# The expert-choice feed-forward of a four-layer decoder: layernorm rows and router products of three token groups moved beside the cross-attention, and the threshold search done on a transposed table

## The chip, the cores and the metric

The kernel is one launch on one core of a Trainium2 chip. The time is the device time of that core in microseconds (us), and lower is better. The core has five engines that run side by side and wait for each other by semaphores: TensorE (PE, with its weight loads as PEld), VectorE (DVE), ScalarE (ACT), GpSimd (POOL) and SyncE (SP, which here only issues transfers). Transfers between the core's memory and the chip's main memory run on 16 DMA engines.

## The reference

The whole program is a decoder of four layers on 16 sequences of 128 tokens (2048 tokens) of width 256. Each layer adds three parts to the running value `x`, each on the layernorm of `x`: a mixer, a cross-attention to a context, and a feed-forward. The change touches the third layer (number 2) only: the end of its cross-attention and its feed-forward, a mixture of 8 experts in which each expert chooses its 256 tokens:

```python
def _L2_ffn_ref(x, Wg, W1, W2):
    B, S, D = x.shape
    E = Wg.shape[1]                 # 8
    T = B * S                       # 2048
    cap = max(1, T // E)            # 256
    xt = x.reshape(T, D)
    logits = xt @ Wg
    probs = jax.nn.softmax(logits, axis=-1)
    pT = probs.T
    _, top_idx = jax.lax.top_k(pT, cap)
    sel = jnp.zeros((E, T), dtype=bool).at[jnp.arange(E)[:, None], top_idx].set(True)
    masked = jnp.where(sel, pT, -jnp.inf)
    assigned = sel.any(axis=0)
    tok2exp = jnp.where(assigned, jnp.argmax(masked, axis=0), jnp.argmax(pT, axis=0))
    weights = jnp.take_along_axis(probs, tok2exp[:, None], axis=1)[:, 0]
    out = jnp.zeros_like(xt)
    for e in range(E):
        gate = jnp.where(tok2exp == e, weights, 0.0)
        h = jax.nn.gelu(xt @ W1[e], approximate=False) @ W2[e]
        out = out + gate[:, None] * h
    return out.reshape(B, S, D)
...
x = x + _L2_xattn_ref(_layernorm(x, axis=-1), ctx_768, ...)     # 8 heads of 64
x = x + _L2_ffn_ref(_layernorm(x, axis=-1), L2_ffn_Wg, L2_ffn_W1, L2_ffn_W2)
```

An expert's choice is the same as a threshold: its 256 largest probabilities are those at or above the 256th largest, with ties settled by the order of the tokens.

## The kernel before

`x` stays on the core in four tiles `x[g]`, one for each group of four sequences (512 tokens: 4 blocks `t` of 128 tokens by 256). The parts of the layers are methods called in order, and a scheduler orders each engine's instructions by their dependences; matrix products issued through `pinned` and `pinned_transpose` (L253 to L258) keep their program order.

The cross-attention `l2_xattn` is `xattn64` (L919) with 8 heads: 16 units `m`, one for each block of tokens. For a unit it issues on PE, all pinned, the column sums `d` of the exponentials of the unit before, the scores `st`, the values `o`, the spread of the reciprocals `rb`, then the maxima's scores `s` of the next unit and the output product `proj` of the unit before the last. `add_x` (L220) adds `proj` to `x`. Every fourth unit a `prologue` makes keys, queries and values of the next group. `xattn64` takes a function `begin`, which is called after the weights are loaded and gives back a table of functions to be called at the ends of units. Layer 1's cross-attention passes `l1_ffn_begin`, which puts layernorm statistics (`stats`), rows (`rows`) and transposes (`turn`) of its feed-forward beside the units in this way. Layer 2's passes nothing.

The feed-forward `l2_ffn` (L1658) runs these stages one after the other:

1. Set-up: 23 transfers of 128 KB write zeros to `hs` in main memory (L1675, queue of SP), and POOL fills constants, among them `bits`, the candidates' bit patterns (L1684).
2. Logits: for each group a layernorm (`norm_tokens`, L194 to L205, rows into `hall`), eight transposes of 128x128 (`tr`, L183), two copies out of PSUM (`hT`, L110 and L112), and for each block two products with Wg (`logits`, L166), which give 8 columns for 128 tokens.
3. Softmax over 8 experts (L1714 to L1721), as `p3`, 128 tokens x (16 blocks x 8 experts).
4. Search: the threshold's bits are found two at a time in 15 rounds. A round makes three candidates for each expert (`cand`, L1732), compares all of `p3` with them (`mask`, L1735: 3 x 16 x 8 = 384 columns), sums over the 128 partitions with a product by ones (`count` on PE), sums over the 16 blocks (`count`, L1743), compares with the capacity (L1744), adds the bits up (`step`, L1746) and sets them (`thr`, L1747). Each step waits for the one before.
5. Selection: `ranks` (L1750) gives each chosen token a running number, with four shifted additions on DVE and two kinds of product on PE; it is called for the tokens above the threshold, for those equal to it, and for the tokens' experts `oh`. What comes out is a row number `at` for each token and an expert for each block of 128 rows.
6. Scatter: 16 indirect transfers on POOL write the rows of `hall` to `hs` (L1827).
7. Blocks: 23 blocks of 128 rows. `fetch` (L1837) reads four blocks of `hs` in one transfer of 512 KB when `b % 4 == 0` (`hb`, L1841, queue of ACT), and an expert's weights for each block (1 MB, queue of SP), into seven buffers of 8 KB per partition (`slot`, L116), which are also those of the cross-attention's weights. Then two transposes (`htr`), the first product, Gelu, four transposes and the second product.
8. Gather: 16 indirect transfers bring the rows back and DVE adds them to `x` (L1902, L1906).

Of the kernel before, what the change touches and what calls it, by code (L numbers as in the profile page):

```python
# [8 lines left out]
F = mybir.dt.float32  # L9
BF = mybir.dt.bfloat16  # L10
U32 = mybir.dt.uint32
AF = mybir.ActivationFunctionType
ALU = mybir.AluOpType
AX = mybir.AxisListType
PSUM = bass.MemoryType.PSUM

P = 128
B = 16
T = B * P
DM = 256  # L20
DC = 192
NG = 4
GB = B // NG
GT = GB * P
# [5 lines left out]
class Decoder:  # L30
# [1622 lines left out]
                add(last, t, po[t] if t < 2 else project(last, t))  # L1653

    def l2_xattn(self):
        self.xattn64(8, [f"L2_xattn_{n}" for n in ("Wq", "Wk", "Wv", "Wout")], "L2_xattn_bout", "l2x")

    def l2_ffn(self):  # L1658

# [2 lines left out]
        nc = self.nc  # L1662
        E, CAP = 8, T // 8
        NB = B + E - 1
        I32 = mybir.dt.int32
        wg = self.wp.tile([P, 2, E], F, tag="wg2", name="wg2")
        self.load_into(wg, "L2_ffn_Wg")
        hs = self.tc.dram_tile([NB * P, DM], F, name="hs")
        ys = self.tc.dram_tile([NB * P, DM], F, name="ys")
        with self.tc.tile_pool(name="l2f", bufs=1) as wk:  # L1670
            tile_ = lambda shape, name, dt=F, bufs=1: wk.tile(shape, dt, tag=name, name=name, bufs=bufs)
            zero = tile_([P, DM], "zero")
            nc.gpsimd.memset(zero, 0.0)
            for b in range(NB):
                nc.sync.dma_start(out=hs[b * P : (b + 1) * P, :], in_=zero)  # L1675
            onesb = tile_([P, P], "onesb", BF)
            nc.gpsimd.memset(onesb, 1.0)
            upb = tile_([P, P], "upb", BF)
            nc.gpsimd.tensor_copy(upb, self.tri["up"])

            bits = tile_([P, 15, 3, E], "bits", I32)
            for i in range(15):
                for j in range(3):
                    nc.gpsimd.memset(bits[:, i, j, :], (j + 1) << (2 * i))  # L1684
            eight = tile_([P, E], "eight")
            for n in range(E):
                nc.gpsimd.memset(eight[:, n : n + 1], float(E - n))
# [9 lines left out]
            for r in ends:  # L1697
                nc.gpsimd.memset(r[:, 0:4], 0.0)

            h = tile_([P, B, DM], "hall")  # L1700
            logits = self.b1("logits")[:, 0 : B * E]
            for g in range(NG):
                hg = h[:, g * GB : (g + 1) * GB, :]
                self.norm_tokens(self.x[g], hg)
                hT = self.hidden_T(hg)
                for t in range(GB):
                    o = (g * GB + t) * E
                    self.mm(logits[:, o : o + E], [(hT[:, k, t * P : (t + 1) * P], wg[:, k, :]) for k in range(2)])

            p3 = tile_([P, B, E], "p3")  # L1710
            flat = lambda a: a.rearrange("p t e -> p (t e)")
            m = self.small([P, B], "m16")
            l3 = logits.rearrange("p (t e) -> p t e", e=E)
            nc.vector.tensor_reduce(m, l3, AX.X, ALU.max)  # L1714
            bcast = lambda a: a.unsqueeze(2).to_broadcast([P, B, E])
            over_t = lambda a: a.unsqueeze(1).to_broadcast([P, B, E])
            nc.vector.tensor_tensor(p3, l3, bcast(m), ALU.subtract)
            nc.scalar.activation(flat(p3), flat(p3), AF.Exp)
            nc.vector.tensor_reduce(m, p3, AX.X, ALU.add)
            nc.vector.reciprocal(m, m)  # L1720
# [1 line left out]

            thr = tile_([P, E], "thr", I32)
            nc.vector.memset(thr, 0)
            cand = tile_([P, 3, E], "cand", I32)
            mask = tile_([P, 3, B, E], "mask", BF)
            count = tile_([P, 3, E], "count")
            step = tile_([P, E], "step", I32)  # L1730
            for i in range(14, -1, -1):
                nc.vector.tensor_tensor(  # L1732
                    cand, bits[:, i], thr.unsqueeze(1).to_broadcast([P, 3, E]), ALU.bitwise_or
                )
                nc.vector.tensor_tensor(  # L1735
                    mask,
                    p3.unsqueeze(1).to_broadcast([P, 3, B, E]),
                    cand.bitcast(F).unsqueeze(2).to_broadcast([P, 3, B, E]),
                    ALU.is_ge,
                )  # L1740
                ps = self.b1("count")[:, 0 : 3 * B * E]
                self.mm(ps, [(onesb, mask.rearrange("p j t e -> p (j t e)"))])
                nc.vector.tensor_reduce(count, ps.rearrange("p (j t e) -> p j e t", j=3, e=E), AX.X, ALU.add)  # L1743
                nc.vector.tensor_scalar(count, count, CAP - 0.5, float(1 << (2 * i)), ALU.is_ge, ALU.mult)  # L1744
                with nc.allow_low_precision(reason="whole numbers of two bits"):
                    nc.vector.tensor_reduce(step, count.rearrange("p j e -> p e j"), AX.X, ALU.add)  # L1746
                nc.vector.tensor_tensor(thr, thr, step, ALU.bitwise_or)  # L1747
            thrf = over_t(thr.bitcast(F))

            def ranks(mask):  # L1750

# [11 lines left out]
            equal = tile_([P, B, E], "equal", BF)  # L1763
            nc.vector.tensor_tensor(above, p3, thrf, ALU.is_gt)
            nc.vector.tensor_tensor(equal, p3, thrf, ALU.is_equal)
            _, n = ranks(above)
            rest = self.small([P, E], "rest8")
            nc.vector.tensor_scalar(rest, n, -1.0, float(CAP), ALU.mult, ALU.add)
            rank, _ = ranks(equal)
# [55 lines left out]
            moves = []  # L1825
            for t in range(B):
                i = nc.gpsimd.indirect_dma_start(  # L1827
                    hs[:, :], bass.IndirectOffsetOnAxis(ap=at[:, t : t + 1], axis=0), h[:, t, :], None
                )
                for j in moves:  # L1830
                    self.tc.declare_no_dep(i.ins, j.ins, reason="the rows of different tokens are different")
                moves.append(i)
# [2 lines left out]
            hbs, hTs, ws, yTs = {}, {}, {}, {}  # L1835

            def fetch(b):  # L1837
                if b % 4 == 0:
                    k = min(4, NB - b)
                    hbs[b // 4] = wk.tile([P, 4, DM], F, tag="hb", name="hb", bufs=3)  # L1840
                    nc.scalar.dma_start(  # L1841
                        out=hbs[b // 4][:, 0:k, :], in_=hs[b * P : (b + k) * P, :].rearrange("(b p) d -> p b d", p=P)
                    )
                e = nc.sync.value_load(ebi[0:1, b : b + 1], min_val=0, max_val=E - 1)
                w = self.slot([P, 2, 1024], "W12")
                w1 = w[:, 0, :].rearrange("p (c f) -> p c f", c=2)
                w2 = w[:, 1, :].rearrange("p (c d) -> p c d", c=4)
                nc.sync.dma_start(
                    out=w1, in_=self.a["L2_ffn_W1"][bass.ds(e, 1)].rearrange("o (c p) f -> p (o c) f", p=P)
                )  # L1850
                nc.sync.dma_start(
                    out=w2, in_=self.a["L2_ffn_W2"][bass.ds(e, 1)].rearrange("o (c p) d -> p (o c) d", p=P)
                )
                ws[b] = w1, w2

            def tokens(b):
                ps = self.b1("htr")[:, 0:DM]
                for k in range(2):
                    self.pinned_transpose(ps[:, k * P : (k + 1) * P], hbs[b // 4][:, b % 4, k * P : (k + 1) * P])
                hTs[b] = wk.tile([P, 2, P], F, tag="hTs", name="hTs", bufs=3)  # L1860
                nc.vector.tensor_copy(hTs[b].rearrange("p c n -> p (c n)"), ps)

# [548 lines left out]
```

## Time and profile before

| What | us |
|---|---|
| Median of 3 runs (3657.71, 3664.07, 3664.17) | 3664.07 |
| The profiled execution's own time | 3659.25 |
| Its span | 3657.5 |
| PE busy | 3343.9 (91% of the span) |
| DVE busy | 2115.8 (58%) |
| ACT busy | 1426.7 (39%) |
| POOL busy | 457.2 (12%) |
| From the last `add_x` of layer 2's cross-attention (2266.37) to the first step of the softmax (2291.68) | 25.31 |
| The 15 rounds of the search (2295.02 to 2333.64) | 38.6 |
| From the end of the search to the row numbers (2346.72) | 13.1 |
| From the row numbers to the first transpose of a block (2374.92) | 28.2 |

The page gives, for one execution, each engine's busy time, the span in 40 slices, the chain of work that ended last, followed back from the end, and groups of equal instructions. Times within the span are us from its start. In the chain and the timeline a row is: start, duration, engine, tile and line, and how many instructions are merged. Durations of PE are modelled, so the start of the next instruction that waits for it is the safer figure. In a table by windows, the columns are the busy time (and number) of PE, PEld, DVE, ACT and POOL, then the TensorE clock that was granted (1.00 is full), the DMA share and GB/s.

### The profile page before, as it was taken

How to read it: one execution, taken by the hardware profiler on the slowest of the kernel's cores; microseconds unless marked ns; L12 is line 12 of the kernel's file. 1: busy time of each engine (PE TensorE's matmuls, PEld its weight loads, DVE VectorE, ACT ScalarE, POOL GpSimd, SP SyncE). 2: the span in 40 equal slices, each digit the busy share in tenths (PEclk: the TensorE clock that was granted, in tenths of full speed). 3: DMA queues.
4: the chain of work that ended last, by engine and by line, in shares of the span. 5: the costliest groups of instructions: out<-in, count | busy, mean ns of one | idle time of the engine just before them, and what ended most of it. 6: DMA issues, size and time to landing. Idle time of an engine off the chain costs nothing.

```text
span 3657.5 us, 51423 instructions
## 1 busy us (share of the span) xinstructions
PE 3343.9 (91%) x20959; PEld 1806.8 (49%) x20976; DVE 2115.8 (58%) x4133; ACT 1426.7 (39%) x1917; POOL 457.2 (12%) x627
## 2 busy tenths in 40 slices
PE   7888999999998899997799999196999999999999
PEld 4655555555556556664455567062122222224656
DVE  6545444444463534468677644425799999973440
ACT  2344411111124422238455422023477777783221
POOL 5423100000003311110010110104100000002100
PEclk9978999999999999999999999597799999999989
DMA  3000000000110100010000001273312020000000
GB/s 98 4 7 1 14 20 20 18 22 18 32 48 2 38 1 1 1 42 8 12 1 12 2 1 34 105 250 107 60 25 31 11 31 11 11 1 25 1 8 18
DMA packets 90484, 105.46 MB, mean 29 GB/s; under 512 B 11364, under 2 KB 72678, under 8 KB 89990
## 3 DMA queue, kind: packets, MB, share of 16 engines
q1 hardware_dynamic: 79672, 89.71, 9.3%
q0 software_dynamic: 4224, 6.43, 0.5%
q10 hardware_dynamic: 6352, 6.03, 0.5%
q8 instruction: 165, 2.70, 0.3%
q14 instruction: 71, 0.58, 0.1%
HBM read 85.53 MB, written 16.60 MB: 28 GB/s over the span
## 4 chain that ended last, share of the span: by engine, by line
PE 79%; DVE 10%; ACT 5%; issue 3%; POOL 2%; DMA 1%; SPq 0%; POOLq 0%; ACTq 0%; DVEq 0%
PE acc L1943 7%; PE down L255 6%; PE gate L255 6%; PE up L255 6%; PE proj L255 6%; PE st L1943 5%; PE one L1943 4%; PE qT L166 4%; PE st L255 4%; PE o L255 2%; PE h L255 2%; DVE mx L2089 2%; PE rb L255 2%; PE v L948 2%; PE pr L166 2%
## 5 line engine op out<-in xcount | busy, mean ns | idle before, releaser
L2089 DVE TENSOR_REDUCE mx<-one 128x1 f32<-128x512 f32 x1024 | 659.0, 686 | 61.8 <-PE one L1943 52.7
L2226 ACT ACTIVATE e<-st 128x1024 f32<-128x1024 f32 x512 | 497.0, 1021 | 214.1 <-PE st L1943 213.0
L674 ACT ACTIVATE gs<-gate,cols 128x512 f32<-128x512 f32 x132 | 90.7, 687 | 552.6 <-PE gate L255 552.6
L1943 PE MATMUL acc<-e,v 128*32 128x512 f32 x2048 | 288.9, 613 | 0.9 <-ACT e L2226 0.9
L1943 PE MATMUL st<-qp,kp 113*128 113x512 bf16 x1024 | 273.8, 388 | 3.4 <-ACT e L2226 1.9
L688 DVE SCALAR_TENSOR_TENSOR x<-down,w_all,x 128x256 f32<-128x256 f32 x512 | 212.4, 477 | 111.1 <-PE down L255 110.9
L255 PE MATMUL down<-expert,gs 128*128 128x256 f32 x1056 | 251.0, 381 | 2.2 <-DVE gs L675 2.2
L255 PE MATMUL gate<-hT,expert 128*128 128x512 f32 x528 | 250.3, 596 | 0.0
L255 PE MATMUL up<-hT,expert 128*128 128x512 f32 x528 | 248.7, 593 | 0.0
L255 PEld LDWEIGHTS down<-expert,gs 128*128 128x128 f32 x1056 | 201.5, 191 | 86.1 <-issue 61.5
L675 DVE SCALAR_TENSOR_TENSOR gs<-up,cols,gs 128x512 f32<-128x512 f32 x132 | 99.0, 750 | 229.8 <-PE up L255 229.8
L1943 PE MATMUL one<-kp,qp 16*128 16x512 bf16 x1024 | 211.7, 399 | 4.0 <-DVE mx L2089 2.6
L1943 PEld LDWEIGHTS <-qp 16*128 16x128 bf16 x1024 | 49.0, 91 | 332.4 <-issue 327.0
L255 PEld LDWEIGHTS up<-hT,expert 128*128 128x128 f32 x528 | 100.8, 191 | 127.1 <-issue 126.9
L1943 PEld LDWEIGHTS <-kp 113*128 113x128 bf16 x1024 | 79.1, 98 | 141.8 <-issue 81.8
L1048 ACT COPY rb<-rb 128x512 f32<-128x512 f32 x64 | 37.5, 586 | 258.9 <-PE rb L255 258.9
L255 PEld LDWEIGHTS gate<-hT,expert 128*128 128x128 f32 x528 | 100.4, 192 | 70.5 <-issue 64.0
L1050 DVE TENSOR_TENSOR cT<-o,rb 128x512 f32<-128x512 f32 x64 | 44.3, 692 | 157.0 <-ACT rb L1048 157.0
L166 PE MATMUL qT<-hT,L_xattn_Wq 128*128 128x512 f32 x256 | 115.8, 606 | 6.6 <-DVE hT L110 4.5
L1346 DVE SCALAR_TENSOR_TENSOR xs<-xBC,cols,xs 128x508 f32<-128x508 f32 x144 | 106.1, 742 | 22.4 <-ACT xs L1342 19.0
L255 PE MATMUL o<-e,v 128*32 128x128 f32 (+1 forms) x2048 | 105.7, 280 | 11.8 <-DVE nm L292 11.8
L962 POOL CAST kb<-kT 128x512 bf16<-128x512 f32 x64 | 41.5, 677 | 433.9 <-DVE kT L110 433.9
(519 smaller groups left out, 5507.9 us busy)
## 6 DMA issues: line engine op xcount, KB each, us to landing
W<-in_L_ffn_W_dram SPq DMA_DIRECT2D x46, 512.0 KB, 5.5
expert<-in_L_ffn_Wg_dram SPq DMA_DIRECT2D x32, 128.0 KB, 2.2
expert<-in_L_ffn_Wu_dram SPq DMA_DIRECT2D x32, 128.0 KB, 2.7
expert<-in_L_ffn_Wd_dram SPq DMA_DIRECT2D x32, 128.0 KB, 2.4
parts<-parts SPq DMA_DIRECT2D x16, 256.0 KB, 2.3
qp<-parts SPq DMA_DIRECT2D x28, 128.0 KB, 3.8
kp<-parts SPq DMA_DIRECT2D x12, 256.0 KB, 8.3
hs<-zero SPq DMA_DIRECT2D x23, 128.0 KB, 1.9
```

Source lines behind the costliest of these rows:

```text
L166: self.nc.tensor.matmul(out, lhsT, rhs, start=i == 0, stop=i == n - 1 and bias is None)
L255: self.tc.keep_in_program_order(self.nc.tensor.matmul(*a, **k))
L674: nc.scalar.activation(gs, pg, AF.Silu, bias=bg)
L675: nc.vector.scalar_tensor_tensor(gs, pu, bu, gs, ALU.add, ALU.mult)
L688: nc.vector.scalar_tensor_tensor(xt, pd[:, t, :], w_all[:, o : o + 1], xt, ALU.mult, ALU.add)
L948: nc.tensor.matmul(ps, l, r, start=True, stop=False)
L962: nc.gpsimd.tensor_copy(kb[:, i + j, :], kT[:, i + j, :])
L1050: nc.vector.tensor_tensor(cT, po, rb, ALU.mult)
L1346: stt = lambda *a: pin(nc.vector.scalar_tensor_tensor(*a))
L1943: self.tc.keep_in_program_order(nc.tensor.matmul(*a, **k))
L2089: nc.vector.tensor_reduce(mx[:, t, kc, i : i + 1], pair[i], AX.X, ALU.max)
L2226: nc.scalar.activation(e[:, 2 * p : 2 * p + 2, :], ps, AF.Exp, scale=1.0 / 16.0)
```

## The change

Three groups' rows and logits move into the cross-attention's units through a new `l2_ffn_begin`; the fourth group follows after it (`st["last"]`). Each group's logits are now made turned: one product with Wg as the stationary operand, padded to 32 columns, gives 32 rows x 512 tokens in `lT`, a strip for each group, and four transposes bring all groups' logits back. The zeroing of `hs` moves there too. `hall` becomes two of the seven 8 KB buffers. The search works on `pT`, the transpose of `p3` (partition = block and expert, columns = 128 tokens): the counts come out of the comparisons themselves (`accum_out`), and one small product with `same` adds up the partitions of one expert. The thresholds come back by a transpose. The first of the three `ranks` becomes one product and one sum. `fetch` reads block 0 alone first, then four at a time. An `Exp` of a constant, whose result is not used, is issued ahead of the softmax.

```diff
     def l2_xattn(self):
-        self.xattn64(8, [...], "L2_xattn_bout", "l2x")
+        self.xattn64(8, [...], "L2_xattn_bout", "l2x", self.l2_ffn_begin)
+
+    def l2_ffn_begin(self):
+        ...
+        wg = self.wp.tile([P, 2, 32], F, tag="wg2", name="wg2")
+        nc.gpsimd.memset(wg, 0.0)
+        nc.sync.dma_start(out=wg[:, :, 0:E], in_=self.a["L2_ffn_Wg"].rearrange("(c p) n -> p c n", p=P))
+        zero = self.hp.tile([P, DM], F, tag="hT", name="zero", bufs=5)
+        nc.gpsimd.memset(zero, 0.0)
+        ...
+        for b in range(NB):
+            nc.sync.dma_start(out=hs[b * P : (b + 1) * P, :], in_=zero)
+        h = [self.slot([P, 8, DM], "hall") for _ in range(2)]
+        ...
+        def stats(gs):
+            ...
+            for i, g in enumerate(gs):
+                for t in range(GB):
+                    nc.vector.bn_stats(bs[:, t, :], self.x[g][:, t, :])
+                    nc.vector.bn_aggr(mv[:, i, t, :], bs[:, t, :])
+            self.rsqrt(rs, mv[:, :, :, 1])
+            ...
+        def rows(g):
+            mv, rs = vals[g]
+            for t in range(GB):
+                nc.vector.tensor_scalar(
+                    h[g // 2][:, g % 2 * GB + t, :], self.x[g][:, t, :], mv[:, t, 0:1], rs[:, t : t + 1], ALU.subtract, ALU.mult
+                )
+
+        def logits(g):
+            hT = self.hp.tile([P, 2, GT], F, tag="hT", name="hT", bufs=5)
+            for k in range(2):
+                ps = self.b1("tr")
+                for t in range(GB):
+                    self.pinned_transpose(ps[:, t * P : (t + 1) * P], h[g // 2][:, g % 2 * GB + t, k * P : (k + 1) * P])
+                self.evac(hT[:, k, :], ps)
+            r = slice(32 * g, 32 * g + 32)
+            ps = self.b1("lT")
+            for k in range(2):
+                self.pinned(ps[r, :], wg[:, k, :], hT[:, k, :], start=k == 0, stop=k == 1)
+            ...
+            nc.scalar.copy(st["lT"][r, :], ps[r, :])
+
+        st["last"] = [lambda: stats([3]), lambda: rows(3), lambda: logits(3)]
+        at = lambda f, *a: lambda: f(*a)
+        return {
+            10: [at(stats, [0, 1]), at(rows, 0)],
+            11: [at(rows, 1), at(logits, 0)],
+            12: [at(logits, 1)],
+            14: [at(stats, [2]), at(rows, 2)],
+            15: [at(logits, 2)],
+        }
...
     def l2_ffn(self):
...
-            bits = tile_([P, 15, 3, E], "bits", I32)
+            bits = tile_([P, 15, 3], "bits", I32)
             for i in range(15):
                 for j in range(3):
-                    nc.gpsimd.memset(bits[:, i, j, :], (j + 1) << (2 * i))
+                    nc.gpsimd.memset(bits[:, i, j : j + 1], (j + 1) << (2 * i))
+
+            m8 = tile_([P, E], "m8")
+            nc.vector.tensor_reduce(m8, self.ident.rearrange("p (t e) -> p e t", e=E), AX.X, ALU.add)
+            same = tile_([P, B, E], "same")
+            nc.gpsimd.tensor_copy(same, m8.unsqueeze(1).to_broadcast([P, B, E]))
...
-            for g in range(NG):
-                hg = h[:, g * GB : (g + 1) * GB, :]
-                self.norm_tokens(self.x[g], hg)
-                hT = self.hidden_T(hg)
-                for t in range(GB):
-                    o = (g * GB + t) * E
-                    self.mm(logits[:, o : o + E], [(hT[:, k, t * P : (t + 1) * P], wg[:, k, :]) for k in range(2)])
+            for work in self.l2f["last"]:
+                work()
+            ...
+            early = self.small([P, 1], "dy")
+            nc.scalar.activation(early, self.eps, AF.Exp)
+            lT = self.l2f["lT"]
+            ps = self.b1("logits")
+            for t in range(GB):
+                self.pinned_transpose(ps[:, t * P : (t + 1) * P], lT[:, t * P : (t + 1) * P])
...
+            ps = self.b1("pT")[:, 0:P]
+            self.pinned_transpose(ps, flat(p3))
+            pT = tile_([P, P], "pT")
+            nc.vector.tensor_copy(pT, ps)
+
+            best = tile_([P, 4], "best")
+            nc.vector.memset(best, 0.0)
+            thr = best[:, 3:4]
...
             for i in range(14, -1, -1):
-                nc.vector.tensor_tensor(
-                    cand, bits[:, i], thr.unsqueeze(1).to_broadcast([P, 3, E]), ALU.bitwise_or
-                )
-                nc.vector.tensor_tensor(mask, p3..., cand..., ALU.is_ge)
-                ps = self.b1("count")[:, 0 : 3 * B * E]
-                self.mm(ps, [(onesb, mask.rearrange("p j t e -> p (j t e)"))])
-                nc.vector.tensor_reduce(count, ps.rearrange("p (j t e) -> p j e t", j=3, e=E), AX.X, ALU.add)
-                nc.vector.tensor_scalar(count, count, CAP - 0.5, float(1 << (2 * i)), ALU.is_ge, ALU.mult)
-                ...
-                    nc.vector.tensor_reduce(step, count.rearrange("p j e -> p e j"), AX.X, ALU.add)
-                nc.vector.tensor_tensor(thr, thr, step, ALU.bitwise_or)
-            thrf = over_t(thr.bitcast(F))
+                nc.vector.tensor_tensor(cand, bits[:, i], thr.bitcast(I32).to_broadcast([P, 3]), ALU.bitwise_or)
+                for j in range(3):
+                    nc.vector.tensor_scalar(
+                        mask, pT, cand.bitcast(F)[:, j : j + 1], 0.0, ALU.is_ge, ALU.add, accum_out=count[:, j : j + 1]
+                    )
+                ps = self.b1("count")[:, 0:3]
+                self.pinned(ps, flat(same), count, start=True, stop=True)
+                nc.vector.scalar_tensor_tensor(best[:, 0:3], ps, CAP - 0.5, cand.bitcast(F), ALU.is_ge, ALU.mult)
+                nc.vector.tensor_reduce(thr, best, AX.X, ALU.max)
+            ps = self.b1("thr")[:, 0:P]
+            self.pinned_transpose(ps, thr.to_broadcast([P, P]))
+            thrf = ps.rearrange("p (t e) -> p t e", e=E)
...
-            _, n = ranks(above)
+            ps = self.b1("above")[:, 0 : B * E]
+            self.mm(ps, [(onesb, flat(above))])
+            n = self.small([P, E], "rest8")
+            nc.vector.tensor_reduce(n, ps.rearrange("p (t e) -> p e t", e=E), AX.X, ALU.add)
...
             def fetch(b):
-                if b % 4 == 0:
-                    k = min(4, NB - b)
+                if b == 0 or b % 4 == 1:
+                    k = min(4, NB - b) if b else 1
```

## The prediction

> **What bounds the kernel now.** The page's first part puts PE at 91% of the span, but its clock row falls to 5 tenths in the slice from 2286 to 2377, which holds most of the change's stages. The chain of waits, asked from 2225 to 2420, shows three regimes. Up to 2266 it is almost all PE: the cross-attention's unit repeats every 6.48 us (starts of `d` at 2142.09, 2148.57, 2155.05), and only one late table load, at 2253.81, adds 0.43. So a PE instruction put there costs its own time. From 2266.37 (last `add_x`) to 2374.92 it runs through one instruction after another, and each removed step pays in full. From 2375 to 2475 it is PE again, at 4.10 us a block; the change alters nothing there but the first fetch.
>
> Chain of waits; the logits of the last group end here, 25.31 us after the last `add_x`:
> ```profile
> 2288.06 3.60 PE logits L166 x16
> 2291.66 0.02 issue
> 2291.68 0.30 DVE m L1714
> ```
> Timeline of one round of the search (start, duration, engine, line). No engine overlaps another, and the next `cand` starts 2.57 us later; 15 rounds are 38.6 us:
> ```profile
> 2299.96 0.18 DVE L1732 TENSOR_TENSOR cand<-bits,thr 128x24 int32<-128x24 int32 x1
> 2300.18 0.56 DVE L1735 TENSOR_TENSOR mask<-p,cand 128x384 bf16<-128x384 f32 x1
> 2300.79 0.48 PE L166 MATMUL count<-mask,onesb 128*128 128x384 bf16 x1 [2.09 <-DVE mask L1735]
> 2301.30 0.56 DVE L1743 TENSOR_REDUCE count<-count 128x24 f32<-128x384 f32 x1 [0.57 <-PE count L166]
> 2301.90 0.18 DVE L1744 TENSOR_SCALAR count<-count 128x24 f32<-128x24 f32 x1
> 2302.11 0.18 DVE L1746 TENSOR_REDUCE step<-count 128x8 int32<-128x24 f32 x1
> 2302.33 0.17 DVE L1747 TENSOR_TENSOR thr<-thr,step 128x8 int32<-128x8 int32 x1
> 2302.53 0.18 DVE L1732 TENSOR_TENSOR cand<-bits,thr 128x24 int32<-128x24 int32 x1
> ```
> PE's timeline in layer 1's cross-attention, where eight pinned transposes stand beside a unit already. From `d` to `d` it is 7.35 instead of 6.48, so 0.87 for eight:
> ```profile
> 1595.99 0.64 PE L255 MATMUL d<-e,pick 128*32 128x128 f32 x16
> ...
> 1602.37 1.04 PE L258 MATMUL tr<-ident,h 128*128 128x128 f32 x8
> ...
> 1603.34 0.64 PE L255 MATMUL d<-e,pick 128*32 128x128 f32 x16
> ```
> Windows after the cross-attention (the third number from the right is the granted clock):
> ```profile
> 2268.00:2269.00 1.00, 0.26 (x3) 0.02 (x1) 1.00 (x1) 0.00 (x0) 1.00 (x32) 1.00 0.53 159
> 2269.00:2270.00 1.00, 0.58 (x2) 0.20 (x2) 1.00 (x4) 0.02 (x1) 0.77 (x12) 0.76 0.44 141
> 2270.00:2271.00 1.00, 0.38 (x2) 0.38 (x2) 1.00 (x3) 0.57 (x1) 0.00 (x0) 0.50 0.34 109
> ```
> ACT's timeline, the kernel's only accumulator outputs, a main row and a read:
> ```profile
> 195.12 0.42 ACT L526 ACTIVATE junk<-qp 128x256 bf16<-128x256 f32 x1 [1.62 <-DVE qp L525]
> 195.44 0.19 ACT L526 ACTIVATION_READ_ACCUMULATOR junk<-qp 128x1 f32 x1
> ```
> Chain again, scatter's landing and the fetch that waits for it:
> ```profile
> 2366.36 4.69 DMA hs<-hall,at
> 2371.07 3.71 DMA hb<-hs
> ```
>
> [...]
>
> **The change, part by part.**
>
> *Beside the cross-attention: +8.8 us.* PE gets, three times, eight transposes (0.87) and four hardware products of 512 columns (`qT`: 16 in 7.13, so 0.43 each, 1.72), and a wait. These are pinned, so `d`, `st` and all of the unit queue behind it: in layer 1 the first copy out of PSUM starts at 1630.42, after `add_x`, and lasts 0.64, while PE is free from 1630.64, so it waits about 0.4. Together 3.0 a group. The last unit already waits 0.47 for a late reciprocal, which the delay hides in part: 2.7. Rows (4 x 0.35) and copies on DVE and ACT lie in idle time (DVE waits 41 us for `rb` over the 16 units); joined statistics drop one table load that a prologue covered. If a copy is held up further, each group costs up to 1 us more; the fewest is the PE work, 7.8. The 23 zero transfers and the memset go some 470 us earlier, SP's queue ahead of the loads of Wv and Wout (1999.87) and POOL's ahead of an addition at 1829.52. In the order as built the memset follows the second `right` (1796.57), and 12.74 us of issuing end before 1815: cost nothing.
>
> *After it: -14.4.* From the last `add_x` at 0: sum for `same` and statistics end at 1.4, but the first `cand` now stands on DVE ahead of the reciprocal and waits for POOL's 45 memsets, which start after the last `proj` and end at 2.3. Reciprocal 2.75, rows 4.2; [...]everything is at half clock. Transposes 0.22 each end at 5.3; four products 3.8 (as in the first block, 2376.10 to 2379.92), 9.1; copy 9.7; four transposes 1.12, 10.9. Before: 25.31. At full clock it would be 2.7 less.
>
> *Softmax: 0.* Its table load (1.28 at 2292.45) should have gone ahead by `early`, but the scheduler puts that `Exp` at the start of layer 2's mixer, where a load for `na` stood anyway.
>
> *Turning: +0.8.* One cold transpose (0.48) and a copy (0.28).
>
> *Search: -2.3.* `cand` 0.21, three comparisons that wait for each other, PE, 0.19, 0.20. [...]ACT's read starts before its main row ends and adds 0.09 (195.63 against 195.54). So 0.38 and 0.02 to the next, 1.20 for three. PE: two hardware pairs, as in two transposes at half clock (2374.92 to 2375.62: 0.70), less about 0.1 for 3 columns, and 0.02: 0.62; the like product at full clock took 0.49 (`wsum`, 1434.10 to 1434.59), and a third pair's time (0.2) more is the upper bound. A round is 2.42 against 2.57; 15 x 0.15. Bounds for the comparison: with the read hidden 0.31 each, 2.15 (-6.3); with a full DVE instruction (0.17) behind it 0.48, 2.66 (+1.4). PE's add -2 and +3.
>
> *Ranks: -0.8.* From the end of the search to `sel` it was 3.86. Now a transpose (0.54), `above`, a product (0.33) and a sum (0.29), then the ranks of `equal`: 3.05.
>
> *First fetch: -1.8.* 128 KB landed in 1.9 for the zeros, against 3.71; among the weight transfers of the blocks as much (`ys`) took 3.9, which would leave no gain, so 0 to -1.8. The next four blocks (512 KB, 4.2) are wanted 5 us later, behind a cold first product. `hall` holds two weight buffers until the scatter; blocks 5 and 6 load after it, needed over 20 us later.
>
> Sum: 8.8 - 14.4 + 0.8 - 2.3 - 0.8 - 1.8 = -9.7. The profiled execution (3659.25: span 3657.5 and 1.75 around it) gives 3649.6. It lies 4.8 below the median; the runs fall in two clusters, and the mean of all four is 3661.3. I predict from that mean: 3651.6.
>
> **Rivals.**
> - *The search gets slower* (ends on the other side): [...]a round is 3.77 and the search +18.0 instead of -2.3; the kernel ends near 3672. The gain is gone at 0.62 a comparison, slower by 0.2% at 0.78. For it: six DVE instructions replace two, and no DVE row shows such a read. Against it: ACT's pair adds 0.09.
> - *PE pays twice beside the cross-attention*: if pinned products wait for copies held behind `nm` (1.22) or the exponentials (1.02), a group costs 5, the cover gives back 6 us, and 3658 is within no change.
> - *A larger gain*: PE keeps full clock behind the last unit (-2.7) and reads hide (-4.0): 3645. [...]
>
> **How the numbers follow.** Measurement of this kernel can tell about 0.2%, 7.3 us, from no change. Forecast, gains of 7.3 to 14: 0.50. Larger gain: 0.20. PE pays twice, or smaller losses together: 0.23. Search slower: 0.07. So faster 0.70, same 0.23, slower 0.07. The range takes in the larger gain with the lower cluster (3645 less 7) and reaches 3662 on the other side.
>
> **What would show it.** In the profile after: `d` to `d` near 9.5 us in the two units after a moved group; the softmax's first step 10.9 us after the last `add_x`, at clock 0.50; a DVE accumulator read behind each comparison and rounds of 2.42; the first `hb` landing in about 2. Rounds over 3.07, or units over 11.5, would make the forecast wrong.

## The result, and the profile after

The changed kernel takes 3644.47 us (median of 20 runs, 3630.46 to 3659.6) against 3658.53 for the kernel before in the same set (20 runs, 3646.43 to 3664.25). The medians lie 14.1 us apart. The ratio over all runs is 0.9966, 95% interval 0.9953 to 0.9979, which is 12.4 us; two later sets gave 0.9945 and 0.9980 (below). The profiled execution has a span of 3637.9 us, 19.6 less than the one before; 4.35 of that lie ahead of the first `d` of layer 2's cross-attention, 2.4 in layer 3, where nothing was changed, and 12.8 between. Line numbers in the views are those of each kernel's own code.

**The units.** PE's timeline after, in two units after each of which one moved group stands (start, duration, engine, line, operation, how many; in brackets PE's idle time and who ended it):

```profile
2233.15 1.16 PE L255 MATMUL st<-qT,kT 64*128 64x128 f32 x16
...
2238.96 1.04 PE L258 MATMUL tr<-ident,hall 128*128 128x128 f32 x8
2240.35 0.62 PE L255 MATMUL lT<-hT,wg 128*32 128x512 f32 x1 [0.35 <-DVE hT L110]
...
2242.62 1.16 PE L255 MATMUL st<-qT,kT 64*128 64x128 f32 x16
```

From `st` to `st` it is 9.47 us instead of 6.48. The transposes, the wait for DVE's copy (0.35) and the products are all seen, in the order in which they were issued. From `d` to `d` it is less, 8.66 and 8.91, because a `d` starts while the products beside it still run.

**The tail**, from the last `add_x` (2270.86) to the softmax. The chain of waits after:

```profile
2271.57 1.50 POOL bits L1742 x45
...
2273.09 0.16 DVE cand L1803
...
2273.38 0.45 DVE hall L1693
...
2273.96 1.21 PE tr L258 x4
...
2275.95 3.39 PE lT L255 x4
...
2279.35 0.59 ACT lT L1710
...
2279.99 0.67 PE logits L258 x4
```

The softmax's first step starts at 2280.68, 9.82 us after the last `add_x`; before it was 25.31. The chain runs through POOL's memsets and the `cand` behind them, as predicted. Windows after, for the same place (busy time of PE, PEld, DVE, ACT, POOL; the third number from the right is the granted clock):

```profile
2274.00:2275.00 1.00, 1.00 (x4) 0.51 (x5) 0.78 (x3) 0.00 (x0) 0.28 (x1) 1.00 0.00 0
...
2277.00:2278.00 1.00, 1.00 (x3) 0.18 (x1) 0.00 (x0) 0.00 (x0) 0.00 (x0) 0.50 0.00 0
...
2279.00:2280.00 1.00, 0.33 (x2) 0.02 (x1) 0.00 (x0) 0.58 (x1) 0.00 (x0) 1.00 0.00 0
```

PE had been idle from 2270.8 to 2273.96, but the clock falls only at 2275.5 (its mean from 2275 to 2276 is 0.76) and is back at 2278.9. So the transposes ran at full clock, and the four products, 0.85 from one start to the next, at half clock except for the last 0.4 us.

**The search.** Timeline after, one round:

```profile
2287.32 0.16 DVE L1803 TENSOR_TENSOR cand<-bits,best 128x3 int32<-128x3 int32 x1
2287.51 0.34 DVE L1805 TENSOR_SCALAR_CACHE_REDUCE mask<-pT,cand 128x128 bf16<-128x128 f32 x1
2287.78 0.08 DVE L1805 DVE_READ_ACCUMULATOR mask<-pT,cand 128x1 f32 x1
2287.90 0.35 DVE L1805 TENSOR_SCALAR_CACHE_REDUCE mask<-pT,cand 128x128 bf16<-128x128 f32 x1
...
2288.70 0.58 PE L255 MATMUL count<-count,same 128*128 128x3 f32 x2 [1.81 <-DVE mask L1805]
2289.32 0.16 DVE L1810 SCALAR_TENSOR_TENSOR best<-count,cand 128x3 f32<-128x3 f32 x1 [0.68 <-PE count L255]
2289.52 0.16 DVE L1811 TENSOR_REDUCE best<-best 128x1 f32<-128x4 f32 x1
2289.71 0.16 DVE L1803 TENSOR_TENSOR cand<-bits,best 128x3 int32<-128x3 int32 x1
```

Each comparison has its accumulator read, which starts 0.27 after the main row, before that row's end. The next comparison starts 0.39 after the one before, and a round is 2.40 instead of 2.57.

**The scatter and the first fetch.** Chain after:

```profile
2352.95 3.37 DMA hs<-hall,at
...
2356.34 2.08 DMA hb<-hs
```

The fetch took 2.08 instead of 3.71, and the scatter's landing 3.37 instead of 4.69.

### The profile page after: what moved, and what is told of

It reads as the page before. It is cut to its first block, busy times and chain, and to the rows that moved or that the text cites. A ratio compares the mean times of both kernels' runs of the same rounds, so it can differ in the third digit from the quotient of the medians.

```text
span 3637.9 us, 51450 instructions
## 1 busy us (share of the span) xinstructions
PE 3329.4 (92%) x20947; PEld 1799.1 (49%) x20947; DVE 2112.6 (58%) x4175; ACT 1425.5 (39%) x1919; POOL 457.3 (13%) x629
## 4 chain that ended last, share of the span: by engine, by line
PE 79%; DVE 10%; ACT 5%; issue 3%; POOL 2%; DMA 1%; SPq 0%; POOLq 0%; ACTq 0%; DVEq 0%
PE acc L2013 7%; PE down L255 6%; PE gate L255 6%; PE up L255 6%; PE proj L255 6%; PE st L2013 5%; PE one L2013 4%; PE qT L166 4%; PE st L255 4%; PE o L255 2%; PE h L255 2%; DVE mx L2159 2%; PE rb L255 2%; PE kT L948 2%; PE v L948 2%
## 5 line engine op out<-in xcount | busy, mean ns | idle before, releaser
L255 PE MATMUL o<-e,v 128*32 128x128 f32 (+1 forms) x2048 | 105.7, 280 | 11.8 <-DVE nm L292 11.8
```

What stands on the lines that cost most here:

```text
L255: self.tc.keep_in_program_order(self.nc.tensor.matmul(*a, **k))
```

## The experiments

All times of a kernel are against the kernel before, run in the same set. Runs of one kernel in one set spread over up to 35 us, and the changed kernel itself gave 0.9966, 0.9945 and 0.9980 in three sets. The lengths of the stages, each from one profile of a kernel, repeat better: in the three profiles of the changed kernel A to D agree within 0.03, S within 0.6 and E within 0.7. So the verdicts below rest on A to D first, and a difference of less than one us in E, F or S says little. What lies outside the stages changes from run to run whatever the kernel: in these profiles the first `d` came between 2099 and 2113, and layer 3 took 1157 to 1173. Stages in us: A from the first `d` of layer 2's cross-attention to the last `add_x`; B from there to the softmax's first step; C the softmax; D from its end to `sel` (turning, search, ranks); E from the last scatter's issue to the first `htr`; F from there to the second block's Gelu; S from the first `d` to layer 3's first transpose.

| Kernel | ratio to before (95%) | A | B | C | D | E | F | S |
|---|---|---|---|---|---|---|---|---|
| before | 1 | 162.69 | 25.31 | 3.30 | 42.50 | 8.56 | 8.82 | 387.59 |
| changed | 0.9966 (0.9953 to 0.9979) | 171.53 | 9.82 | 3.30 | 40.09 | 5.60 | 8.07 | 374.75 |
| x_place | 0.9951 (0.9938 to 0.9964) | 162.69 | 14.47 | 3.30 | 40.08 | 5.45 | 8.59 | 370.88 |
| x_search | 0.9987 (0.9975 to 0.9999) | 171.52 | 10.14 | 3.31 | 41.33 | 5.45 | 7.74 | 375.79 |
| x_fetch | 0.9971 (0.9959 to 0.9983) | 171.53 | 9.81 | 3.31 | 40.09 | 8.75 | 8.21 | 378.13 |
| x_early | 0.9976 (0.9964 to 0.9988) | 171.53 | 9.15 | 2.03 | 40.06 | 5.48 | 7.85 | 372.42 |
| x_form | 0.9984 (0.9969 to 0.9998) | 162.68 | 20.25 | 3.31 | 40.15 | 5.48 | 7.74 | 375.98 |
| x_pipe | 0.9941 (0.9927 to 0.9956) | 162.69 | 11.34 | 2.03 | 40.35 | 5.70 | 8.76 | 367.31 |
| x_warm | 0.9949 (0.9934 to 0.9964) | 162.69 | 11.35 | 2.02 | 40.90 | 9.05 | 6.24 | 368.56 |
| x_after | 0.9945 (0.9925 to 0.9966) | 171.54 | 9.79 | 3.31 | 40.09 | 5.21 | 8.26 | 374.54 |
| x_fill | 0.9958 (0.9942 to 0.9974) | 171.53 | 8.35 | 3.31 | 40.10 | 5.72 | 8.77 | 374.09 |
| x_best | 0.9943 (0.9923 to 0.9964) | 162.69 | 11.34 | 2.03 | 38.03 | 6.84 | 7.36 | 364.49 |
| x_best2 | 0.9941 (0.9922 to 0.9961) | 162.70 | 11.34 | 2.03 | 38.07 | 6.85 | 6.01 | 363.25 |
| x_after2 | 0.9980 (0.9968 to 0.9992) | 171.54 | 9.81 | 3.30 | 40.11 | 5.88 | 8.06 | 375.06 |

**x_place: no group beside the cross-attention.**

```diff
-        st["last"] = [lambda: stats([3]), lambda: rows(3), lambda: logits(3)]
-        return {10: [...], 11: [...], 12: [...], 14: [...], 15: [...]}
+        st["last"] = [at(stats, [0, 1]), at(rows, 0), at(rows, 1), at(logits, 0), at(logits, 1)]
+        st["last"] += [at(stats, [2]), at(rows, 2), at(logits, 2), at(stats, [3]), at(rows, 3), at(logits, 3)]
+        return {}
```

> All four groups' statistics, rows, transposes and products stand after the cross-attention; the turned logits, the search and the rest are as in the changed kernel. Theory (the place pays): layer 2's cross-attention, from its first d to the last add_x, goes back from 171.5 us to 162.7, and from the last add_x to the softmax's first step it becomes about 26 instead of 9.8, because four turned products of 0.86 at half clock (3.4) cost what sixteen of 0.22 cost before (3.5), with a copy and four transposes of 1.3 behind them. Kernel about 7 us slower than the changed one, 5 faster than before. Rival (the form pays): turned products alone shorten the logits; the stage ends near 13 without being moved, and the kernel is some 6 us faster than the changed one.

A went back by 8.84 as expected, but B became 14.47 and not 26: S is 3.9 *shorter* than in the changed kernel. So the theory fell; the place does not pay. PE's timeline of x_place in the tail (last `add_x` at 2264.27):

```profile
2264.07 1.04 PE L258 MATMUL tr<-ident,hall 128*128 128x128 f32 x8
2265.64 1.90 PE L255 MATMUL lT<-hT,wg 128*32 128x512 f32 x4 [0.54 <-DVE hT L110]
2267.48 1.09 PE L258 MATMUL tr<-ident,hall 128*128 128x128 f32 x8
2268.92 1.90 PE L255 MATMUL lT<-hT,wg 128*32 128x512 f32 x4 [0.35 <-DVE hT L110]
```

PE goes on without a gap behind the last `proj`, since the rows of groups 0 to 2 had been written during the units (`hall` lies in buffers that are there by then). It stays at full clock (1.00 in all windows from 2264 to 2278), four products take 1.90, and a group costs 3.28. Meanwhile DVE makes group 3's statistics and rows, for which PE waits 3.1 us in the changed kernel. Moving three groups saves 4.65 after the cross-attention and costs 8.84 in it.

**x_form: x_place with the logits' form of before.**

```diff
-                self.pinned(ps[r, :], wg[:, k, :], hT[:, k, :], start=k == 0, stop=k == 1)
+                    self.pinned(lg[:, o : o + E], hT[:, k, t * P : (t + 1) * P], wg[:, k, 0:E], ...)
```

> As x_place (all four groups after the cross-attention, their first three groups' rows written during it), but the logits are formed as before, by sixteen products of 8 columns with the turned rows as weights, pinned, without the copy of lT and the four transposes back. Theory (the turned form pays nothing; what paid is that the rows lie in the weights' buffers, so that DVE writes them early, and that PE stays busy and at full clock): sixteen products at full clock take half of the 3.5 us that they took before, the same 1.8 as four turned ones, and the stage from the last add_x to the softmax's first step is 14.5 less a copy and four transposes, 13.2. Rival (the turned form pays): sixteen weight loads keep 0.22 each even then, a group costs 1.7 more, and the stage is near 20.

Both were half right. B is 20.25, the rival's number, but the sixteen products cost no more than four turned ones as long as the clock is full. PE's timeline and two windows of x_form:

```profile
2276.64 1.95 PE L255 MATMUL logits<-wg,hT 128*128 128x8 f32 x16 [0.54 <-DVE hT L110]
2278.44 1.88 PE L258 MATMUL tr<-ident,hall 128*128 128x128 f32 x8
2280.26 3.90 PE L255 MATMUL logits<-wg,hT 128*128 128x8 f32 x16
```

```profile
2277.00:2278.00 1.00, 1.00 (x12) 1.00 (x11) 0.30 (x2) 1.00 (x1) 1.00 (x27) 1.00 0.00 0
...
2282.00:2283.00 1.00, 1.00 (x7) 1.00 (x6) 0.00 (x0) 0.00 (x0) 0.00 (x0) 0.50 0.00 0
```

The first group's sixteen take 1.95. Then the clock falls (at 2278.5), although from the first of these products on PE and its weight loads show as busy without a gap, and stays at 0.50 for the other three groups. In x_place, with the same order and the same gaps up to there, it stays at 1.00. So in this pair of profiles products of 8 columns let the clock fall where products of 512 hold it; why is not settled here. Taken in this order, the gain of 15.5 thus splits into 5.1 for what else is new in the tail (25.31 to 20.25), 5.8 for the turned form with the clock that it keeps (to 14.47), and 4.65 for the place (to 9.82), the only one that has a price. The 5.1 were not separated by runs: rows written early, joined statistics, a pinned order. But the traces show that 2.9 of them lie ahead of the first group's products. These start 1.38 after the last `add_x` in x_form and 4.25 after it in before (2270.62), where DVE writes no row until 2266.71.

**x_search: the search and its bits as before, the rest changed.**

```diff
-            for i in range(14, -1, -1):
-                nc.vector.tensor_tensor(cand, bits[:, i], thr.bitcast(I32).to_broadcast([P, 3]), ALU.bitwise_or)
-                ...
-            self.pinned_transpose(ps, thr.to_broadcast([P, P]))
+            for i in range(14, -1, -1):
+                nc.vector.tensor_tensor(cand, bits[:, i], thr.unsqueeze(1).to_broadcast([P, 3, E]), ALU.bitwise_or)
+                ...
+            thrf = over_t(thr.bitcast(F))
```

> The changed kernel with the search and the count of ranks of before (three masks of 128x384, reduced after the product), the rest as changed. Theory: rounds go back from 2.40 to 2.57, the search from 35.9 to 38.6, the turning (1.0) goes, from the search's end to sel it is 3.84 or, with the changed ranks kept, 3.1 less the transpose of thr, 2.5; together +1.2 to +2.4 us against the changed kernel, which the times hardly show and the stages do. Rival: most of the tail's gain of 20.9 us comes from the turned search; then the stage between the last add_x and the first htr is 10 us or more longer than in the changed kernel.

D is 41.33 instead of 40.09: the turned search is worth 1.24 with its turning, as the theory had it; the rival fell. The time (0.9987) lies 0.2% above the changed kernel's first set, more than 1.24 us; but no stage of the trace shows the rest, and the changed kernel's own sets differ by as much, so it is not put down to the search.

**x_fetch: four blocks in the first fetch.**

```diff
-                if b == 0 or b % 4 == 1:
-                    k = min(4, NB - b) if b else 1
+                if b % 4 == 0:
+                    k = min(4, NB - b)
```

> The changed kernel with the first fetch of four blocks (512 KB), as before. Theory: it lands in about 3.7 us instead of 2.1, the first htr comes 1.6 later, and the landing of the scatter stays at 3.4. Rival 1: the landing is set by the weights beside it, it stays near 2 and nothing is gained by the small fetch. Rival 2: the scatter's landing (4.7 before, 3.4 after) belongs to the fetch too, and goes back to 4.7; then the small fetch is worth 2.9.

Rival 2 was right. Chain of x_fetch, and SP's timeline: its tenth to twelfth weight transfers, of which the eleventh is the one at 2352.21:

```profile
2356.41 4.67 DMA hs<-hall,at
...
2361.10 3.92 DMA hb<-hs
```

```profile
2350.15 0.37 SPq L1921 DMA_DIRECT2D W<-in_L_ffn_W_dram  x1
2352.21 0.38 SPq L1918 DMA_DIRECT2D W<-in_L_ffn_W_dram  x1
2365.04 0.37 SPq L1921 DMA_DIRECT2D W<-in_L_ffn_W_dram  x1
```

The scatter's landing went back to 4.67 and the fetch to 3.92. The two parts are separate, as the other kernels show. In before, x_fetch, x_warm, x_best and x_best2 the eleventh weight transfer is issued 2 to 5 us ahead of the last scatter's issue, and the landing takes 4.5 to 4.7. In the changed kernel, x_place, x_search, x_early, x_pipe, x_fill, x_after and x_after2 it is issued only after the first fetch has landed, and the landing takes 2.9 to 3.7 (x_form's trace does not show its landing). The fetch of one block itself takes 2.1 beside an early eleventh transfer too (x_best: landing 4.55, fetch 2.14). So the smaller fetch is worth 1.6 to 1.8. The other 1.3 go with a transfer of weights that is held back past the scatter, in all thirteen profiles that show the landing; no run held that transfer back by itself, so that it is the cause is likely and not shown, and why it is held back stays open.

**x_early: the idle `Exp` behind the last reciprocal, the bits set early.**

```diff
-            early = self.small([P, 1], "dy")
-            nc.scalar.activation(early, self.eps, AF.Exp)
...
+            if gs == [3]:
+                nc.scalar.activation(self.small([P, 1], "dy"), rs[:, 0, 0:1], AF.Exp)
```

> The changed kernel with the idle Exp made to depend on the last group's reciprocal, so that its table load can't go ahead to the mixer and falls between the last square root and the copies, and with the 45 memsets of the candidates' bits issued before layer 0. Theory: from the end of p's subtraction to the start of the Exp 1.45 becomes about 0.2 (-1.2), and the last rows start 0.65 earlier, since the reciprocal no longer stands behind a cand that waits for POOL. Together -1.9 us between the last add_x and the search. Rival: the load collides with the copies of hT on ACT (second copy at 4.8 us after the last add_x) and gives back most of it; or the rows come earlier but the products stay at half clock for as long, and the start of the softmax moves by less than 0.3.

ACT's timeline of x_early:

```profile
2284.06 1.28 ACT L1694 ACT_TABLE_LOAD   x1
2285.36 0.20 ACT L1694 ACTIVATE dy<-l1rs 128x1 f32<-128x1 f32 x1
2286.53 0.59 ACT L112 COPY hT<-tr 128x512 f32<-128x512 f32 x1 [0.97 <-PE tr L258]
...
2292.39 0.31 ACT L1785 ACTIVATE p<-p 128x128 f32<-128x128 f32 x1 [1.53 <-DVE p L1784]
```

The load and the `Exp` are over 0.97 before the next copy starts. B fell by 0.67 and C by 1.27, as the theory said. The rival fell. The time does not show the 2 us.

**x_pipe: x_place with transposes ahead of products, the early `Exp`, and the first round without `cand`.**

```diff
+        st["last"] += [at(turned, 0), at(turned, 1), at(logits, 0), at(turned, 2), at(logits, 1)]
+        st["last"] += [at(turned, 3), at(logits, 2), at(logits, 3)]
```

> As x_place, with PE's order in the tail changed (transposes of group g+1 ahead of the products of group g, so that PE need not wait for the copies: 0.84 idle in each of the four groups), with the idle Exp tied to the last reciprocal, and the first round's comparisons reading the bits themselves instead of a cand. Theory: the stage from the last add_x to the softmax's first step goes from 14.5 to about 12.5 (three waits of 0.84 less 0.3 of new ones), the Exp starts 1.2 earlier as in x_early, the rest is as in x_place: 3.2 us less in all. Rival: the last group's rows become the bound (statistics, square root and rows end 5.9 after the last add_x, then transposes, copy and products): 0.2, 1.1, 0.7, 1.9, 0.6, 0.7 behind that are 11.1, so 12.5 stays possible only if the products of group 2 are done by then; else up to 14.

B is 11.34, 1.2 less than expected. PE's timeline of x_pipe:

```profile
2276.04 1.90 PE L255 MATMUL lT<-hT,wg 128*32 128x512 f32 x4
2277.87 1.09 PE L258 MATMUL tr<-ident,hall 128*128 128x128 f32 x8
2278.90 2.39 PE L255 MATMUL lT<-hT,wg 128*32 128x512 f32 x8
```

Eight products of two groups end 2.39 after their start where four take 1.90. Their outputs lie in different strips of 32 partitions, and they overlap: 2.39 for two groups beside 1.90 for one. C falls to 2.03 as in x_early, and S is 3.6 less than in x_place. Leaving out the first `cand` brought nothing: D is 0.27 longer, and the first round's comparisons, which now read `bits`, start 0.48 apart instead of 0.39.

**x_warm, x_best, x_best2: idle products to keep the clock up.** x_pipe with products ("idle" below) whose results nobody reads, in the softmax, in each round and ahead of the first block. The excerpt shows x_best; x_warm has 384 columns in a round and ten products ahead of the block. All three also call `fetch` for three blocks (x_warm: four) before the first block.

```diff
                 self.pinned(ps, flat(same), count, start=True, stop=True)
+                for _ in range(3):
+                    self.pinned(warm[:, 0:256], self.ident, self.ctx0[:, 0:256], start=True, stop=True)
...
+            for _ in range(8):
+                self.pinned(warm, self.ident, ws[2][1].rearrange("p c d -> p (c d)")[:, 0:512], ...)
```

> x_pipe with products whose result nobody reads, to keep PE's clock up: six of 512 columns during the softmax, three of 384 columns in each round of the search while DVE compares, and ten of 512 columns after the last rank's product, once the weights of block 3 have landed. Theory: the search's own product falls from 0.59 to about 0.3 at full clock, a round from 2.40 to 2.12, the search by 4.2; transposes of pT and thr by 0.2 each; from the first htr to the first y 5.0 becomes 2.9. Together 6 to 7 us less than x_pipe. Rival: the clock does not rise, three products of 0.65 at half clock fill more than the 1.8 us that PE has, each round is 0.2 to 0.8 longer, and the kernel is 3 to 12 us slower than x_pipe.

In x_warm the idle products of a round, six hardware products of 384 columns, took 2.18; four of 512 take 1.90 at a clock of 1.00 (x_place), so the clock was full there too, by this estimate. But a product of 512 f32 columns is two hardware products of 0.43 (the eight that the code issues for `lT` are 16 in the changed kernel's trace, with starts at 2240.80, 2241.23 and 2241.66), so the idle ones were twice as long as planned. Those in the softmax held up `pT` by 2.5, those in a round (2.18) set its length, 2.19, and those of the last round held up the transpose of `thr` by 1.4. Those before the first block ran on to 2364.5, 4.5 behind the scatter's landing. S is 1.3 more than in x_pipe, where 6 to 7 less was expected.

> x_pipe with idle products sized by what x_warm showed (a product of 512 f32 columns takes 0.86 at full clock, twice what was assumed there): two of 512 and one of 256 columns in the softmax, three of 256 in each round, and eight of 512 once the weights of block 2 have landed. Theory: nothing waits for them any more, a round falls from 2.40 to 2.13 and the search by 4.1, thr and pT by 0.2 each, the first block by 1.9 and the second by 0.7; 7 us less than x_pipe, 27 less than before. Rival: three products of 256 columns (1.3 of 2.1 us) are too little to keep the clock up, the rounds stay at 2.40, and only the first block gains.

Rounds of x_best and the end of its search, PE's timeline:

```profile
2286.45 0.38 PE L255 MATMUL count<-count,same 128*128 128x3 f32 x2 [0.41 <-DVE mask L1813]
2286.69 1.54 PE L255 MATMUL warm<-ctx,ident 128*128 128x256 f32 x6
2288.64 0.39 PE L255 MATMUL count<-count,same 128*128 128x3 f32 x2 [0.41 <-DVE mask L1813]
...
2310.83 1.54 PE L255 MATMUL warm<-ctx,ident 128*128 128x256 f32 x6
2312.21 0.27 PE L258 MATMUL thr<-ident,best 128*128 128x128 f32 x1
```

In these rounds nothing waits for the idle products now, and `count` takes 0.39 instead of 0.58, not the 0.3 expected: a round is 2.19. Two places still wait. One early round took 2.68 (2281.68 to 2284.36), since the clock was at half there (`count` 0.57, the six idle products behind it 2.42 instead of 1.54) and the next `count` stood behind them. After the last round the transpose of `thr` stands behind them too: it starts 0.85 after DVE has set `thr` (2311.36), instead of 0.06 in x_pipe. So D falls by 2.3 instead of 4.5: 2.7 in the search, less 0.6 behind it. E is 1.1 longer, with the scatter's landing at 4.55 again. S is 2.8 less than in x_pipe, not 7. In the first block the clock fell once more (mean 0.54 from 2352 to 2354), and the first product took 3.33.

> x_best with nine instead of eight idle products ahead of the first block, since in x_best they ended 1.4 before the first htr and the clock fell once more at its first product (3.33 instead of 1.9). Theory: they end just before the landing, the first product takes 1.9, from the first htr to the first y 4.3 becomes 2.9 and to the second y 3.1 stays; some 12 us less than the changed kernel by stages, and as much in the times of this set. Rival: the end of the idle products comes behind the landing and delays htr by up to 1.7, or the clock falls all the same, and nothing is gained against x_best; then 10 us less than the changed kernel.

Nine products end 0.43 before the first `htr`, the first product of x_best2 takes 1.98 instead of the 3.78 of before, and F is 6.01, as the theory had it. S is 24.3 less than before.

**x_after and x_after2: the changed kernel again.**

> The changed kernel once more, beside the two others of this set. By its stages it should be 12.0 to 12.8 us faster than before (0.33 to 0.35%), with 171.5 us from the first d of layer 2's cross-attention to the last add_x, and 87.7 from there to the first htr. If the gain of 12 us came from other stages by chance, the ratio should go towards 1.

> The changed kernel beside x_best2 on one chip, since the times of one kernel from set to set differ by more than the stages do (0.9966 and 0.9945 so far). If the stages are right, its ratio to before is near 0.9966 and x_best2 is 0.3% below it; if the whole-kernel times hide the stages' differences, the two ratios overlap.

The stages repeat (S 374.54 and 375.06), the times don't: 0.9945 from only 6 runs, and 0.9980 from 20. In neither does the interval reach 1. In the last set x_best2 (0.9941, 8 runs) lies below the changed kernel (0.9980), and their intervals don't meet: it beats both before and the changed kernel, the latter by 11.8 in S.

**x_fill: three idle products ahead of the last group's transposes.**

```diff
+            for _ in range(3):
+                self.pinned(warm, self.ident, self.ctx0[:, 0:512], start=True, stop=True)
             for work in self.l2f["last"]:
                 work()
```

> The changed kernel with three products of 512 columns, whose result nobody reads, between the last projection and the last group's transposes, where PE stood idle 3.1 us. Theory [...]: they keep the clock full, the four turned products take 1.9 instead of 3.4, and the stage from the last add_x to the softmax's first step falls from 9.8 to 8.3. Rival (the fall has another cause, such as the long stretch at full load before): the products stay at 0.86 each, and the stage stays at 9.8 or grows to 10.3.

B is 8.35. PE's timeline of x_fill:

```profile
2277.67 1.64 PE L258 MATMUL tr<-ident,hall 128*128 128x128 f32 x8 [0.57 <-DVE hall L1693]
2279.65 1.90 PE L255 MATMUL lT<-hT,wg 128*32 128x512 f32 x4 [0.35 <-DVE hT L110]
```

The theory held: with most of the idle time ahead of the transposes filled, the four products take 1.90 instead of the 3.37 of the changed kernel. So it is this idle time that halved the clock behind it, and it costs 1.5. S fell only by 0.7, because the clock came back later in the first blocks (F 8.77; the second block's first product takes 2.18, in the changed kernel 1.88). What sets the moment of such a change is not shown. The traces show how far apart the changes lie: in the changed kernel they come at 2275.52, 2278.94, 2282.35 and 2364.27, so 3.42, 3.41 and 81.92 apart, the last 24 times 3.413; in before at 2269.53 and 2382.17, 112.64 apart, 33 times 3.413. F lies between 7.7 and 8.8 in eleven profiles whose blocks are alike. It grows with the time from the first `htr` to the return of the clock, in the same order in all eleven: 7.74 where it came back after 4.2 (x_form), 8.07 after 5.7 (changed), 8.82 after 7.2 (before). None of these eleven moved that return on purpose.

## Why the prediction was right or wrong

The forecast (faster, by 9.7 in its sum) came true, and the time lies in the range. Of the 7.1 us by which 3644.5 lies below the 3651.6, 2.8 are the base (3658.5 for before in that set, where 3661.3 was taken), 3.1 are terms of the sum, and 1.2 the scatter of the times. Two gains, 1.32 and 0.75, had no term in the sum; that they came on top was luck. Point by point:

- *Beside the cross-attention, +8.8:* measured 8.84, and a unit of 9.47 where 9.5 was named (from `st` to `st`; from `d` to `d`, as it was named, 8.66 and 8.91). The wait for the copy was 0.35 for 0.4. Rival "PE pays twice" fell.
- *After it, -14.4:* measured -15.49. The term was too small by 1.1. Some 0.9 of it is the clock, which the working put, by estimate, at half for the whole stage: the four products took 3.40 instead of 3.8, since it was back for their end, and from the last transposes to the softmax it was 0.69 instead of 1.2. The first transposes, at full clock, waited only for rows. The other 0.2 was there when the products began (5.09 for 5.3): POOL's memsets ended at 2.2, where 2.3 was said, and the rows at 3.92 for 4.2. The larger gain (clock full throughout) was there to be had: x_fill shows its 1.5.
- *Softmax 0:* C is 3.30 in both; the table load (1.28) stands in the chain, as said.
- *Turning, +0.8:* 1.03.
- *Search, -2.3:* -2.73, from 38.62 to 35.89 (2285.05 to 2320.94). A round is 2.40 for 2.42, a comparison 0.39 for 0.40, and the first round has no `cand` ahead of it. Rival "the search gets slower" (rounds of 3.77) fell: a read starts before its main row ends.
- *Ranks, -0.8:* -0.7.
- *First fetch, -1.8:* -1.63 for the fetch. The scatter's landing, -1.32, was in no step: the working looked at which weights load after the scatter, not at which transfer is still under way at its end (x_fetch).
- *Blocks:* 0.75 less in the second block, because the clock came back 5.7 us after the first `htr` and not 7.2; chance, since F of the same blocks lies anywhere from 7.7 to 8.8.

These add up to the 12.8 by which S fell. What the prediction did not ask is whether its two largest terms belong together. It set +8.8 against -14.4 as one move. The runs showed that 10.8 of the 15.5 come without moving any group's products (x_place): 5.8 with the turned products, 5.1 with what else is new in the tail. The move alone loses 4.2.

## What to carry to other kernels

Cost the alternative of leaving a piece where it is in its *new* form before crediting a move with the whole gain: here a group cost 2.99 in the full stage and 3.28 in the tail, and one that stays covers another's latency. Where PE waits for short chains on other engines, look at the granted clock by windows, and see what the late engine could be given instead. When a whole-kernel time scatters by 0.3% and the change is as small, lengths between two named instructions of the trace decide sooner than more runs.

## What had not been expected of the hardware

- Products of 8 columns with full weight loads were followed by a fall of PE's clock to 0.50 while the records show PE busy at 1.00 (x_form, 2277 to 2280), and it stayed at 0.50 to the end of the stage (2295); with products of 512 columns in the same places it stayed at 1.00 (x_place).
- In the changed kernel's tail PE's clock fell 4.7 us after the last product before the gap (2270.8 to 2275.5), when the next instructions had been running for 1.5. In before it fell at 2269.53, 0.16 after the start of the next instructions, though PE's gaps there were of 1.04 and 1.11 only. So it fell behind short gaps too, and in neither trace within a gap.
- A `tensor_scalar` of 128 f32 columns with an accumulator output takes 0.35, where the working had 0.29, which before's `above` took, a `tensor_tensor` of that size (L1764; a plain `tensor_scalar` of it, `never_b`, takes 0.22), its read 0.08, and the pair 0.39 from start to start.
- Two turned products with outputs in different strips of 32 partitions overlap: eight in 2.39 instead of 3.7, which is twice the 1.83 from the first of one group's products to what follows them (x_pipe). In the units, where `d` and `lT` overlap too, this saved nothing that could be seen: from the first `lT` to `st` 2.27, and four products with a `d` of 0.57 are 2.29.
